# The last block of a four-layer cross-attention stack: outputs projected into rows, and the last unit's denominators partly on TensorE

## The chip, the cores and the metric

The kernel runs on one core of one Trainium2 chip. The metric is the device time of one execution in microseconds; the median of three runs is given. Beside it there is one profiled execution, whose span runs from the first to the last instruction.

## The reference

Four layers of multi-head cross-attention are applied one after the other to `x` (1 x 2048 queries x 256), with keys and values from a context of 1601 rows x 512. All is in float32.

```python
# layers L0, L2, L3: 16 heads of 64, two pairs of key columns with a bias from masks
q, k, v = hidden @ Wq, ctx @ Wk, ctx @ Wv            # split into heads
logits = einsum('bhqd,bhkd->bhqk', q, k) * 64 ** -0.5 + col_bias
out = softmax(logits) @ v                             # heads joined again: 1024 columns
x = out @ Wo + bo + x
# layer L1: 16 query heads of 16 on 4 key heads, on the rms-normed x, no bias
x = x + attention(rmsnorm(x) @ wq, ctx @ wk, ctx @ wv) @ wo
```

The output is `x` after L3.

## The kernel before

The sequences are held transposed: `xs` is x in SBUF with the 256 channels on partitions (two halves of 128) and the 2048 queries along the free dimension. The queries are cut into four query blocks b = 0 to 3 of 512 (`QB`, each `QT` = 4 pieces of 128), the keys into 13 chunks (`NT`) of 128 (the last has 65).

A layer with masks has 8 blocks of two heads (n = 0 to 7), the grouped layer L1 has 4 of four heads. One block and one query block make a `Unit`; there are 112, in the order layer, block, query block. Units 108 to 111 are the last block (layer 3, n = 7), and unit 111 is the very last. Each unit adds its heads' share of `out @ Wo` to `xs`.

A unit goes through stages, a chunk of keys at a time:
- `masked_scores` (L675): the two heads' scores of a chunk on TensorE into a pair of PSUM banks, which ScalarE copies to `p` (L687) while VectorE keeps a running maximum `top` (L692).
- `maxima` (L735, L736): after 13 chunks `top` is transposed by TensorE and reduced; `on_all_partitions` (L643, L646) sends the result to DRAM and back, spread over all partitions. `maxima_spread` copies it to the PSUM tile `b` (L751).
- `subtract` (L756, VectorE) and `masked_exp` (L761, ScalarE), in place in `p`; GpSimd adds `p` to `sums` chunk by chunk (L764 for the first, L766 for the rest).
- `values` (L801): the products of `p` with the values, summed over the chunks in the PSUM bank `po`; both heads lie in it, 64 partitions each. At the end `po` is copied to `oT` (L806).
- `denominators` (L822, L826, L827): `sums` is transposed in 8 pieces of 128 x 128 on TensorE, reduced and inverted on VectorE, and spread through DRAM into `by`. `divide` (L842, GpSimd) multiplies `oT` with it.
- `project` (L850): two products with `wo` into a pair of banks, which VectorE adds to `xs` (L862, or L857 with the bias `bo` in the layer's last block).
- After the last block `rows_out` transposes `xs` of a query block back into rows (L619), copies half on ScalarE and half on VectorE (L622, L623), and issues two output DMAs from SP (L625).

The order of work is written out by hand. A step is one chunk of one unit, and steps are taken in pairs. At step s, unit k scores chunk c where s = 13k + c; it exponentiates 18 steps later and takes the values 20 steps later. So at any time one unit is scored while the one before it is exponentiated. Shorter jobs are `Piece`s: `pieces.at(step, found)` puts them at a step, counted from a unit's last value chunk (step 13k + 32). Denominators come 2 steps later, division 5, projection 10 and `rows_out` 11. In the last block there are no projections of a next block to fill in between.

The instructions of TensorE, ScalarE and VectorE are tied to the order in which they are written. PSUM has two pair buffers (`psum.pair`), a third of the same size (`psum.b`), one bank `pm` and one bank `po`. Whatever wants a pair buffer waits until the reader of the one before last has finished. Unit 110's `sums`, `oT` and pieces share the engines with the exponentials of unit 111, behind which nothing more is scored.

Of the kernel before, what the change touches and what calls it, by code (L numbers as in the profile page):

```python
# [10 lines left out]
FP = mybir.dt.float32  # L11
# [3 lines left out]
ALU = mybir.AluOpType  # L15
# [3 lines left out]
P = 128  # L19
QB = 512  # L20
# [6 lines left out]
Piece = namedtuple("Piece", "run cost shared", defaults=(True,))  # L27
# [7 lines left out]
def tile_cross_attention_stack(ctx: ExitStack, tc: tile.TileContext, t: dict, out: bass.AP):  # L35
# [31 lines left out]
    nc = tc.nc  # L67
    x, cond = t["x"], t["ctx_2048"]
    _, S, C = x.shape
    _, T, CT = cond.shape  # L70
    NQ = S // P
    NC = C // P
    NCT = CT // P
    NB = S // QB
    QT = QB // P
    TCH = spans(T, P)
    NT = len(TCH)
# [3 lines left out]
    masked_names = ["L0_xattn_", "L2_xattn_", "L3_xattn_"]  # L81

    NP = 22
    const = ctx.enter_context(tc.tile_pool(name="const", bufs=1))
    weights = ctx.enter_context(tc.tile_pool(name="weights", bufs=2))
    heads = ctx.enter_context(tc.tile_pool(name="heads", bufs=2))
    probs = ctx.enter_context(tc.tile_pool(name="probs", bufs=NP))
    work = ctx.enter_context(tc.tile_pool(name="work", bufs=2))
# [3 lines left out]
    ps_m = ctx.enter_context(tc.tile_pool(name="ps_m", bufs=1, space=PSUM))  # L92
    scores_pools = ctx.enter_context(ExitStack())

    ident = const.tile([P, P], FP, name="ident")
    make_identity(nc, ident)
    ones = const.tile([P, P], FP, name="ones")
# [32 lines left out]
    psum = Scores()  # L130
# [3 lines left out]
    xs = const.tile([P, NB, NC, QB], FP, name="xs")  # L134
    x_rows = [probs.tile([P, QT, C], FP, name="p") for _ in range(NB)]
    for b in range(NB):
        nc.scalar.dma_start(
            out=x_rows[b], in_=x[0, ts(b, QB), :].rearrange("(n p) c -> p n c", p=P)
# [102 lines left out]
    def width(c):  # L241

        return sum(m for _, m in TCH[c : c + 2])

    def context_slice(c, held):

        a = TCH[c][0]
        n = width(c)
        ct = work.tile([P, NCT, 2 * P], FP, name="ct", bufs=3)
        nc.sync.dma_start(out=ct[:, :, :n], in_=ctxT_dram[:, :, a : a + n])  # L250
        held[c] = lambda k: ct[:, k, :n]
# [139 lines left out]
    class Masked:  # L391
# [5 lines left out]
        def __init__(self, l):  # L397
            self.l, self.name = l, masked_names[l]
# [59 lines left out]
    class Grouped:  # L458
# [5 lines left out]
        name = "L1_xattn_"  # L464
# [106 lines left out]
    layers = [Masked(0), Grouped(), Masked(1), Masked(2)]  # L571
# [11 lines left out]
    def keep(l, b):  # L583
        nc.sync.dma_start(out=xT_dram[l][b], in_=xs[:, b])
# [26 lines left out]
            (12, Piece(rms, 1.5)),  # L611
        ]

    def rows_out(b):

        pt = psum.pair((QT, C))
        for q in range(QT):
            for k in range(NC):
                nc.tensor.transpose(pt[:, q, ts(k, P)], xs[:, b, k, ts(q, P)], ident)  # L619
        rows = work.tile([P, QT, C], FP, name="ct", bufs=3)  # L620
        half = QT // 2
        nc.scalar.copy(rows[:, :half, :], pt[:, :half, :])  # L622
        nc.vector.tensor_copy(rows[:, half:, :], pt[:, half:, :])  # L623
        for q0 in (0, half):
            nc.sync.dma_start(  # L625
                out=out[0, b * QB + q0 * P : b * QB + (q0 + half) * P, :].rearrange(
                    "(n p) c -> p n c", p=P
                ),
                in_=rows[:, q0 : q0 + half, :],
            )  # L630

    def columns(q):

# [3 lines left out]
    def on_all_partitions(cols, to):  # L637


        n = cols.shape[1]  # L640
        rows = dram.tile([4, P, QT], FP, name="cols", bufs=4)[:n]
        with nc.allow_non_contiguous_dma(reason="1024 values, four at a time"):
            nc.sync.dma_start(out=rows.rearrange("h p q -> p h q"), in_=cols)  # L643
        for tile_, heads_ in to:
            src = rows[heads_].rearrange("(o h) p q -> o (h p q)", o=1)
            nc.sync.dma_start(out=tile_, in_=src.to_broadcast(tile_.shape))  # L646


    class Unit:
        def __init__(self, l, u, b, sub):  # L650
            self.l, self.u, self.b, self.sub = l, u, b, sub
            self.layer = u.layer
            self.pair = self.layer.SUBS[sub]
            self.masked = isinstance(self.layer, Masked)
            self.p = [None] * NT

        def rows(self, h):
            size = P // len(self.pair)
            return slice(size * h, size * h + size)
# [98 lines left out]
        def masked_exp(self, c):  # L758
            m = TCH[c][1]
            p = self.p[c]  # L760
            nc.scalar.activation(p[:m], p[:m], AF.Exp)  # L761
            if c == 0:
                self.sums = work.tile([P, 2, QB], FP, name="sums")
                nc.gpsimd.tensor_copy(self.sums, p)  # L764
            else:
                nc.gpsimd.tensor_tensor(self.sums[:m], self.sums[:m], p[:m], ALU.add)  # L766

        def scores_again(self, c, h, s):
# [17 lines left out]
        def values(self, c, part=None):  # L786


            u = self.u
            _, m = TCH[c]  # L790
            if c == 0 and not part:
                self.po = ps_o.tile([P, QB], FP, name="po")
            for h in range(len(self.pair)):
                r = self.rows(h)
                if self.masked:
                    to, v, p = self.po[r, :], u.v[:m, c, r], self.p[c][:m, h, :]
                else:
                    at = ts(part, QB // 2)
                    to, v = self.po[r, at], u.v[:m, c, :]
                    p = self.p[c][h // 2][:m, h % 2, at]  # L800
                nc.tensor.matmul(  # L801
                    to, v, p, start=(c == 0 and not part), stop=(c == NT - 1 and part != 0)
                )
            if c == NT - 1 and part != 0:
                self.oT = work.tile([P, QB], FP, name="oT", bufs=1)
                nc.scalar.copy(self.oT, self.po)  # L806

        @property
# [35 lines left out]
        def project(self):  # L844

            k = 0
            for py in psum.heads(False):
                of = range(k, k + py.shape[1])
                for k in of:
                    nc.tensor.matmul(  # L850
                        py[:, k - of[0], :], self.u.wo[:, ts(k, P)], self.oT, start=True, stop=True
                    )
                k += 1
                if self.masked and self.u.n == self.layer.BLOCKS - 1:
                    for j in of:
                        bo, to = bo_of[self.layer.l][:, j : j + 1], xs[:, self.b, j, :]
                        nc.vector.scalar_tensor_tensor(  # L857
                            to, py[:, j - of[0], :], bo, to, ALU.add, ALU.add
                        )
                else:  # L860
                    to = xs[:, self.b, of[0] : k, :]
                    nc.vector.tensor_tensor(to, py, to, ALU.add)  # L862

        def finish(self):

            last = 10 if self.masked else 8
            return [
                (2 if self.masked else 3, Piece(self.denominators, 1.0, not self.masked)),
                (5, Piece(self.divide, 0.0)), (last, Piece(self.project, 2.0, False)),
            ]  # L870
# [7 lines left out]
    units = []  # L878
# [4 lines left out]
    of = {}  # L883
# [14 lines left out]
    for i in range(NK):  # L898
        ct = first_context_slice(i)
# [63 lines left out]
    pieces = Pieces()  # L963

    def start_block(i):

        if i + 1 == len(blocks):
            return
        l, n = blocks[i + 1]
        layer = layers[l]  # L970
        nxt = made[l, n] = layer.load(n)

        loads, held = deque(), {}

        def chunks(make, cost):
            def piece(c):
                make(c, held[c])
                if loads:
                    loads.popleft()()

            loads.extend(lambda c=c: context_slice(c, held) for c in range(0, NT, 2))
            return [Piece(lambda c=c: piece(c), cost(c)) for c in range(0, NT, 2)]

        makers = layer.projections(nxt)
        first, second = [], []
        if makers:
            first = chunks(makers[0], lambda c: width(c) / P)
            second = chunks(makers[1], lambda c: float(len(TCH[c : c + 2])))
            for _ in range(3):
                loads.popleft()()  # L990
        first += layer.own_keys(nxt)
        second += layer.own_values(nxt)

        grouped = i and not isinstance(layers[blocks[i - 1][0]], Masked)
        (pieces.later if grouped else pieces.fill).extend(first)
        pieces.later.extend(second)

    def after(k):

        i, b, _ = units[k]  # L1000
        l, n = blocks[i]
        if n + 1 < layers[l].BLOCKS or not of[k].last:
            return []
        if l + 1 == len(layers):
            return [(11, Piece(lambda: rows_out(b), 1.0))]
        if isinstance(layers[l + 1], Masked):
            return [(11, Piece(lambda: keep(l + 1, b), 0.0))]
        return norm_factors(l + 1, b)
# [176 lines left out]
```

## Time and profile before

| what | value |
|---|---|
| median of 3 runs | 4948.83 us (4944.98 to 4951.98) |
| profiled execution | 4952.0 us, span 4950.3 us, mean granted TensorE clock 0.977 |
| busy, PE | 4747.6 us (96%) |
| busy, DVE | 3752.7 us (76%) |
| busy, ACT | 3218.1 us (65%) |
| busy, POOL | 2988.8 us (60%) |
| last score (L675) of unit 111 ends | 4875.3 us |
| last exponential (L761) ends | 4912.3 us |
| last addition to `sums` (L766) ends | 4927.7 us |

PE is TensorE's matmuls, PEld its weight loads, DVE VectorE, ACT ScalarE, POOL GpSimd, and SP the engine that issues nearly all DMAs. A float32 matmul has two records in the trace and a transpose one, so a projection of two products is "x4". Times in the trace count from the span's start. "L801" is a line of the kernel as printed above. The brackets at the end of a timeline row give the engine's idle time before the row and what ended it.

### The profile page before, as it was taken

What the parts mean: (1) busy time and instruction counts of PE and PEld (TensorE: products, weight loads), DVE (VectorE), ACT (ScalarE), POOL (GpSimd) and SP (SyncE); (2) the same over time, 40 slices, a digit from 0 to 9 for tenths busy, and PEclk for the clock granted to TensorE, in tenths of its full rate; (3) what the DMA queues carried; (4) which work ended last, traced back from release to release, by engine and by line L of the source; (5) the groups of instructions that cost most, each with busy time, mean ns of one, the idle gap of its engine ahead of it and who ended that gap; (6) DMA issues with size and microseconds to landing.
All of it is one profiled execution on the core that took longest, in us unless ns stands there. A gap on an engine that the chain in (4) does not pass through costs nothing.

```text
span 4950.3 us, 64060 instructions
## 1 busy us (share of the span) xinstructions
PE 4747.6 (96%) x24004; PEld 2061.6 (42%) x24004; DVE 3752.7 (76%) x3782; ACT 3218.1 (65%) x4000; POOL 2988.8 (60%) x1429
## 2 busy tenths in 40 slices
PE   6899999999999999999999999999999999999996
PEld 4344444444444444444344444444444444444432
DVE  3788888888765666554378888888888888888886
ACT  2677777777634555444467777777777777777774
POOL 1677777777720000000177777777777777777787
PEclk9999999999989999999799999999999999999998
DMA  4222222222201000012133232232222322223211
GB/s 140 65 79 81 80 83 82 81 85 75 71 26 37 19 19 19 26 29 59 29 91 87 77 86 79 82 88 77 78 85 84 84 82 78 79 83 86 78 29 34
DMA packets 352534, 337.88 MB, mean 68 GB/s; under 512 B 120697, under 2 KB 306297, under 8 KB 352224
## 3 DMA queue, kind: packets, MB, share of 16 engines
q1 hardware_dynamic: 348960, 328.41, 23.5%
q8 instruction: 189, 3.10, 0.3%
q0 software_dynamic: 1152, 3.28, 0.2%
q10 hardware_dynamic: 2112, 2.10, 0.1%
q14 instruction: 121, 0.99, 0.1%
HBM read 318.89 MB, written 14.82 MB: 67 GB/s over the span
## 4 chain that ended last, share of the span: by engine, by line
PE 85%; DVE 10%; issue 1%; POOL 1%; ACT 1%; DMA 1%; SPq 0%; POOLq 0%; DVEq 0%; ACTq 0%
PE po L801 27%; PE s L675 19%; PE t L706 8%; PE pm L381 6%; PE pm L427 6%; PE s L850 4%; PE pm L451 4%; PE t L771 3%; DVE rden L826 2%; DVE ntop L736 2%; PE s L822 2%; DVE xs L862 2%; PE s L735 2%; DVE top L692 1%; DVE p L756 1%
## 5 line engine op out<-in xcount | busy, mean ns | idle before, releaser
L766 POOL TENSOR_TENSOR sums<-sums,p 128x1024 f32<-128x1024 f32 (+1 forms) x1152 | 2726.6, 2367 | 754.0 <-ACT p L761 582.2
L687 ACT COPY p<-s 128x1024 f32<-128x1024 f32 (+1 forms) x1248 | 1235.0, 1014 | 680.5 <-PE s L675 590.5
L801 PE MATMUL po<-p,v 128*64 128x512 f32 (+3 forms) x8320 | 1512.2, 531 | 10.4 <-ACT p L761 6.7
L756 DVE TENSOR_TENSOR p<-p,b 128x1024 f32<-128x1024 f32 (+1 forms) x1248 | 1460.9, 1209 | 56.1 <-ACT b L751 54.9
L692 DVE TENSOR_TENSOR top<-s,top 128x1024 f32<-128x1024 f32 (+1 forms) x1056 | 1290.6, 1222 | 233.0 <-ACT p L687 169.6
L675 PE MATMUL s<-q,kT 64*128 64x512 f32 (+1 forms) x4992 | 1348.5, 634 | 91.8 <-DVE ntop L736 23.7
L761 ACT ACTIVATE p<-p 128x1024 f32<-128x1024 f32 (+1 forms) x1248 | 1254.9, 1057 | 51.7 <-DVE p L756 50.3
L801 PEld LDWEIGHTS po<-p,v 128*64 128x64 f32 (+3 forms) x8320 | 368.0, 126 | 1106.3 <-issue 865.3
L675 PEld LDWEIGHTS s<-q,kT 64*128 64x128 f32 (+1 forms) x4992 | 390.6, 182 | 741.8 <-issue 210.2
L783 ACT ACTIVATE p<-t 128x512 f32<-128x512 f32 (+1 forms) x760 | 412.3, 594 | 414.8 <-PE t L706 377.5
L719 DVE TENSOR_REDUCE row_top<-t 128x1 f32<-128x512 f32 x700 | 451.0, 686 | 260.4 <-PE t L706 257.7
L842 POOL TENSOR_TENSOR oT<-oT,by 128x512 f32<-128x512 f32 x112 | 142.9, 1275 | 764.5 <-DMA by<-cols 423.6
L706 PE MATMUL t<-kT,q 32*128 32x512 f32 (+1 forms) x1880 | 562.6, 642 | 0.0
L771 PE MATMUL t<-q,kT 32*128 32x512 f32 (+1 forms) x1520 | 493.7, 662 | 0.0
L706 PEld LDWEIGHTS t<-kT,q 32*128 32x128 f32 x1880 | 294.9, 316 | 168.8 <-issue 84.3
L381 PEld LDWEIGHTS pm<-wv,ct 128*128 128x128 f32 (+1 forms) x2496 | 290.2, 188 | 130.7 <-issue 71.2
L381 PE MATMUL pm<-wv,ct 128*128 128x128 f32 (+2 forms) x2496 | 322.5, 282 | 6.9 <-ACT v L385 3.2
L427 PE MATMUL pm<-ct,wk 128*128 128x256 f32 (+1 forms) x1288 | 301.1, 377 | 0.6 <-DMA wk<-in_L_xattn_Wk_dram 0.6
L736 DVE TENSOR_REDUCE ntop<-s 128x8 f32<-128x1024 f32 x96 | 117.5, 1224 | 229.0 <-PE s L735 229.0
L427 PEld LDWEIGHTS pm<-ct,wk 128*128 128x128 f32 x1288 | 221.0, 190 | 150.0 <-issue 93.6
L764 POOL COPY sums<-p 128x1024 f32<-128x1024 f32 x96 | 99.5, 1036 | 203.2 <-ACT p L761 203.2
L850 PE MATMUL s<-oT,wo 128*128 128x512 f32 x392 | 199.6, 632 | 17.5 <-POOL oT L842 13.6
(155 smaller groups left out, 2356.2 us busy)
## 6 DMA issues: line engine op xcount, KB each, us to landing
ct<-ctxT SPq DMA_DIRECT2D x288, 512.0 KB
xT<-xT SPq DMA_DIRECT2D x100, 512.0 KB
spread<-cols SPq DMA_DIRECT2D x96, 512.0 KB
by<-cols SPq DMA_DIRECT2D x192, 128.0 KB
xT<-xs SPq DMA_DIRECT2D x16, 512.0 KB
ct<-ctxT SPq DMA_DIRECT2D x48, 130.0 KB
wk<-in_L_xattn_Wk_dram SPq DMA_DIRECT2D x24, 256.0 KB
wv<-in_L_xattn_Wv_dram SPq DMA_DIRECT2D x24, 256.0 KB
```

The lines of the kernel that those rows point to most:

```text
L381: nc.tensor.matmul(pv[:md, d, :f], ct(k)[:, d * P : d * P + md], wv[:, k, :], start=(k == 0), stop=(k == NCT - 1),)
L427: nc.tensor.matmul(pk, u.wk[:, k, :], ct(k), start=(k == 0), stop=(k == NCT - 1))
L675: nc.tensor.matmul(s[:m, h, :], self.u.kT[r, a : a + m], self.q[r, :], start=True, stop=(a != TAIL),)
L687: nc.scalar.copy(p[:m], s[:m])
L692: nc.vector.tensor_tensor(self.top[:m], s[:m], self.top[:m], ALU.max)
L706: nc.tensor.matmul(s[:, at : at + n], self.q[r, columns(q)], self.u.kT[r, a : a + n], start=True, stop=True,)
L719: nc.vector.tensor_reduce(self.top[:, of, q, k : k + 1], s, AX.X, ALU.max)
L756: nc.vector.tensor_tensor(self.p[c][:m], self.p[c][:m], self.less[:m], ALU.add)
L761: nc.scalar.activation(p[:m], p[:m], AF.Exp)
L766: nc.gpsimd.tensor_tensor(self.sums[:m], self.sums[:m], p[:m], ALU.add)
L771: nc.tensor.matmul(s[:m], self.u.kT[r, a : a + m], self.q[r, :], start=True, stop=True)
L801: nc.tensor.matmul(to, v, p, start=(c == 0 and not part), stop=(c == NT - 1 and part != 0))
```

## The change

In the last block the residual is no longer updated in `xs`. For query blocks 0, 1 and 2, `rows_of_x` transposes `xs` into rows early in the block (steps 1406, 1416, 1442 as counted from the block's first step 1404) and ScalarE copies all of it. `project_rows` then takes `oT` as the stationary operand, so that its products (128 queries x 256 channels each) come out as rows; VectorE adds them to the rows, and two DMAs write them out. The bias `bo` of layer 3 is added one block earlier.

The very last unit differs more. GpSimd adds only chunks 0 to 5 to `sums`. For chunks 6 to 12, and at the end for `sums`, TensorE multiplies with a block of ones and adds up in the bank `pm` (`dens`), which gives the denominators on all partitions without a transpose or a trip through DRAM. `x_below` (step 1465) puts the rows of `xs` into PSUM with an identity product, where the projection is added later. `quarters` (step 1475, that of the last value chunk) inverts, multiplies, projects, copies and writes 128 queries at a time; between the multiplications and the projections it does the row projection of unit 110, which has been taken out of its place.

```diff
+    LAST_ADDED = 6
...
-    def rows_out(b):
+    def rows_of_x(b):
         pt = psum.pair((QT, C))
         for q in range(QT):
             for k in range(NC):
                 nc.tensor.transpose(pt[:, q, ts(k, P)], xs[:, b, k, ts(q, P)], ident)
-        rows = work.tile([P, QT, C], FP, name="ct", bufs=3)
-        half = QT // 2
-        nc.scalar.copy(rows[:, :half, :], pt[:, :half, :])
-        nc.vector.tensor_copy(rows[:, half:, :], pt[:, half:, :])
-        for q0 in (0, half):
-            nc.sync.dma_start(
...
+        x_rows_of[b] = work.tile([P, QT, C], FP, name="ct", bufs=3)
+        nc.scalar.copy(x_rows_of[b], pt)
+    x_rows_of = {}
+    def rows_out(b, rows, q, n):
+        nc.sync.dma_start(
+            out=out[0, b * QB + q * P : b * QB + (q + n) * P, :].rearrange(
+                "(n p) c -> p n c", p=P
+            ),
+            in_=rows[:, q : q + n, :],
+        )
...
+            self.final = self.l == len(layers) - 1 and u.n == self.layer.BLOCKS - 1
+            self.very_last = self.final and b == NB - 1
+            self.added = LAST_ADDED if self.very_last else NT
...
-            else:
+            elif c < self.added:
                 nc.gpsimd.tensor_tensor(self.sums[:m], self.sums[:m], p[:m], ALU.add)
...
+            if self.masked and self.very_last:
+                if c == 0:
+                    self.dens = ps_m.tile([P, QB], FP, name="pm")
+                todo = [self.p[c]] if c >= self.added else []
+                if c == NT - 1:
+                    todo.append(self.sums)
+                for p in todo:
+                    k = m if p is self.p[c] else P
+                    for h in range(2):
+                        nc.tensor.matmul(
+                            self.dens[self.rows(h), :], ones[:k, :64], p[:k, h, :],
+                            start=(c == self.added), stop=(p is self.sums),
+                        )
             if c == NT - 1 and part != 0:
-                self.oT = work.tile([P, QB], FP, name="oT", bufs=1)
+                if self.masked and self.very_last:
+                    self.oT = work.tile([P, 2, QB], FP, name="spread", bufs=1)[:, 0, :]
+                else:
+                    self.oT = work.tile([P, QB], FP, name="oT", bufs=1)
                 nc.scalar.copy(self.oT, self.po)
...
-                if self.masked and self.u.n == self.layer.BLOCKS - 1:
+                if self.masked and self.u.n == self.layer.BLOCKS - 1 - (self.l == len(layers) - 1):
...
+        def project_rows(self, py=None):
+            py = py or psum.pair((QT, C))
+            for q in range(QT):
+                nc.tensor.matmul(
+                    py[:, q, :], self.oT[:, ts(q, P)], self.u.wo, start=True, stop=True
+                )
+            rows = x_rows_of[self.b]
+            nc.vector.tensor_tensor(rows, py, rows, ALU.add)
+            for q in (0, QT // 2):
+                rows_out(self.b, rows, q, QT // 2)
+        def x_below(self):
+            pairs = [psum.pair(), psum.pair()]
+            self.py = [pairs[q // 2][:, q % 2, :C] for q in range(QT)]
+            for q in range(QT):
+                for k in range(NC):
+                    nc.tensor.matmul(
+                        self.py[q][:, ts(k, P)], xs[:, self.b, k, ts(q, P)], ident,
+                        start=(k == 0), stop=False,
+                    )
+        def quarters(self, before):
+            rden = work.tile([P, NC, QB], FP, name="xT")[:, 0, :]
+            for q in range(QT):
+                nc.vector.reciprocal(rden[:, ts(q, P)], self.dens[:, ts(q, P)])
+                nc.gpsimd.tensor_tensor(
+                    self.oT[:, ts(q, P)], self.oT[:, ts(q, P)], rden[:, ts(q, P)], ALU.mult
+                )
+            before.project_rows(psum.b().rearrange("p a (b c) -> p (a b) c", c=C))
+            rows = work.tile([P, QT, C], FP, name="ct", bufs=3)
+            for q in range(QT):
+                nc.tensor.matmul(
+                    self.py[q], self.oT[:, ts(q, P)], self.u.wo, start=False, stop=True,
+                )
+                nc.scalar.copy(rows[:, q, :], self.py[q])
+                rows_out(self.b, rows, q, 1)
         def finish(self):
+            if self.very_last:
+                return [(0, Piece(lambda: self.quarters(of[len(units) - 2]), 2.0))]
+            if self.final:
+                found = [
+                    (2, Piece(self.denominators, 1.0, False)), (5, Piece(self.divide, 0.0)),
+                ]
+                if self.b < NB - 2:
+                    found.append((10 - 2 * self.b, Piece(self.project_rows, 2.0, False)))
+                return found
...
     def start_block(i):
         if i + 1 == len(blocks):
+            start = units.index((i, 0, 0)) * NT
+            for b, at in enumerate((2, 12, 38, NB * NT + 9)):
+                piece = Piece(lambda b=b: rows_of_x(b), 1.0, False)
+                if b == NB - 1:
+                    piece = Piece(lambda: of[len(units) - 1].x_below(), 2.0, False)
+                pieces.at(start + at, [(0, piece)])
             return
...
         if l + 1 == len(layers):
-            return [(11, Piece(lambda: rows_out(b), 1.0))]
+            return []
```

More of the change, by code (lines that the diff above doesn't have):

```diff
@@ L619, in rows_out @@
                 nc.tensor.transpose(pt[:, q, ts(k, P)], xs[:, b, k, ts(q, P)], ident)
-        rows = work.tile([P, QT, C], FP, name="ct", bufs=3)
-        half = QT // 2
-        nc.scalar.copy(rows[:, :half, :], pt[:, :half, :])
-        nc.vector.tensor_copy(rows[:, half:, :], pt[:, half:, :])
-        for q0 in (0, half):
-            nc.sync.dma_start(
[L626 to L630, printed above, removed]
+        x_rows_of[b] = work.tile([P, QT, C], FP, name="ct", bufs=3)
[8 more added lines that the diff above has]
+        )
     def columns(q):
```

## The prediction

> **What bounds the kernel now.** I read the granted clock first (0.977, one core), then the slices of the page: PE is at 9 tenths in all 40 but the first two and the last, so what ends the span must be looked for in the last slices. A table of stretches near the end (its columns: length, then the busy time of PE, weight load, DVE, ACT and POOL with the number of instructions, granted clock, DMA share, GB/s):
>
> ```profile
> 4860.00:4880.00 20.00, 16.38 (x74) 5.64 (x70) 18.40 (x17) 14.99 (x16) 15.41 (x8) 1.00 0.08 17
> 4880.00:4900.00 20.00, 13.77 (x58) 4.19 (x58) 14.71 (x14) 11.79 (x13) 18.67 (x10) 1.00 0.19 53
> 4900.00:4920.00 20.00, 12.86 (x43) 3.39 (x41) 10.81 (x11) 9.17 (x9) 19.53 (x9) 0.83 0.05 13
> 4920.00:4951.00 31.00, 11.18 (x36) 5.67 (x36) 5.24 (x8) 1.75 (x3) 8.76 (x5) 0.61 0.13 43
> ```
>
> DVE leads until 4880 (18.40 of 20), POOL from there to 4928 (19.53 of 20), and after that no engine is busy for half the time. The chain of waits says the same in order (start, length, what):
>
> ```profile
> 4925.40 2.35 POOL sums L766
> 4927.79 2.00 PE s L822 x8
> 4929.81 1.24 DVE rden L826
> 4931.30 2.53 DMA cols<-rden
> 4934.39 2.89 DMA by<-cols
> 4938.76 3.80 PE s L850 x4
> 4944.04 1.77 PE s L619 x7
> ```
>
> So the end is two pieces. POOL adds up the last unit's thirteen chunks (one copy, then 2.4 us each) until 4927.74, although its last exponential was there at 4912.3. Then nine dependent links take 4950.3 - 4927.8 = 22.5 us: transposes, reduction, a trip of the denominators through DRAM (6.1 us), division, projection, transposes, two copies, write. The timeline of the same end:
>
> ```profile
> 4894.40 0.69 DVE L623 COPY ct<-s 128x512 f32<-128x512 f32 x1 [1.60 <-ACT ct L622]
> 4897.45 17.07 POOL L766 TENSOR_TENSOR sums<-sums,p 128x1024 f32<-128x1024 f32 x7 [0.52 <-ACT p L761]
> 4900.77 1.22 DVE L826 TENSOR_REDUCE rden<-s 128x8 f32<-128x1024 f32 x1 [1.17 <-PE s L822]
> 4904.47 6.74 PE L801 MATMUL po<-p,v 128*64 128x512 f32 x24 [1.86 <-ACT p L761]
> 4915.79 3.78 PE L850 MATMUL s<-oT,wo 128*128 128x512 f32 x4 [4.59 <-POOL oT L842]
> ```
>
> The third matters too: the next-to-last unit's projection (L850) waits for its division on POOL, and the last unit's value products stand behind it in PE's order.
>
> **The Trainium skill.** Its page TensorE: Matmul & The Clock Gate (section "Part 1: The HAM clock gate (the "warmup" mystery)") says that TensorE falls to half clock after an idle window of some 3.4 us. The trace agrees: after an idle stretch of 4.6 us the four records of L850 take 3.78 us, not 1.98. TensorEngine Tiling (Array Packing) (section "Overview") says that products with 64 output columns can run two at a time; here the two heads' L801 products, four records, take 1.94/2 = 0.94 to 0.97 us a chunk in a run of two chunks, while one full-width product of the same length takes 1.98/2 = 0.99 (L850). VectorE: DVE Perf Modes ("First, the fixed hardware budget") has the reciprocal as an iterated division, repeated 8 times. The trace agrees that it is slow for each element:
>
> ```profile
> L605 DVE RECIPROCAL rms<-rms 128x4 f32<-128x4 f32 x4 | 0.7, 178 | 1.1 <-ACT rms L604 1.1
> L827 DVE RECIPROCAL rden<-rden 128x8 f32<-128x8 f32 x96 | 19.5, 203 | 3.3
> L834 DVE RECIPROCAL rden<-pm 128x16 f32<-128x16 f32 x16 | 4.1, 257 | 34.3 <-PE pm L831 34.3
> ```
>
> From 4 to 16 elements 178 to 257 ns: 6.6 ns each. A 128x128 one is thus 257 + 112 x 6.6 = 1.0 us, no shape of the trace. Below it can't be under the 0.2 us of L827; above, 8 cycles an element at the page's 0.96 GHz (its section "Specifications") and 0.15 start give an estimate of 1.2. I take 1.0.
>
> **Part 1, ahead of the end.** Three `rows_of_x` calls go in at steps 1406, 1416, 1442: 8 transposes (1.1 us, L619), one ACT copy of 1024 (1.01, L687), and one of the two pair buffers held for both. At 1406 they stand before the projection L850, which then waits: its buffer comes at 4741.7 and not 4740.5, DVE's update follows, +1.25. At 1416 and 1442 they stand before the transposes of the maxima (L735), for which DVE already waits 1.57 us: +1.15 each. Sum +3.6; 0 if PE's gaps take them, 6.3 if copy and transposes add up each time. ACT has 5 us free in 20, so its copy delays no exponential much.
>
> The bias goes into block n=6's projections: two DVE operations of 0.70 in place of one of 1.22, +0.2 for the three that fall in the DVE-led last block, +0.6 (0 to 0.8).
>
> Query block b=0's write-out at step 1447 goes. DVE there waited 1.69 us for ACT's half, copied 0.69 and its update was 0.2 longer: -2.5, of which I take -2.4. Its four row products have as many columns as the two of L850 that they replace. Its two output DMAs move a step ahead; SP's next DMA behind them is issued 11 us later, so they cost nothing. Net by 4879: +1.8.
>
> Query block b=1 goes from steps 1459/1460 to 1457. Before, DVE idled 1.91 us for L850 and spent 1.41; now the update (1.22) stands between chunks 9 and 10 with a wait of some 0.4. That is -1.7, so the last subtraction of b=2 ends at 4890.5, as before. Then the stall and copy of L623 (DVE 4892.8 to 4895.0) are gone too: chunks 1 to 4 are subtracted by 4897.2, not 4899.6. SP: b=1's output DMAs go behind those of the last maxima, already under way.
>
> **Part 2, the last unit.** POOL ends b=2's sums at 4895.9 + 1.8 = 4897.7 (it had no gap from 4877 on, so it keeps the delay). L822 1.2, reduction and reciprocal 1.4: 4900.3. `x_below` wants both pair buffers, one of them free only then: 16 records of 128 columns cost 2.05 us (L381 has the same shape), half before, half after: PE free at 4901.2. Behind it wait the value products of chunks 3 to 12.
>
> From there PE has 10 chunks of values and 8 pairs of `dens` products (chunks 6 to 12 and `sums`), of L801's shape: 18 x 0.935 (1.87 a pair of chunks in the chain) = 16.8 us, **T0 = 4918.0**. DVE subtracts chunks 5 to 12 by 4909.4 and ACT is 1.1 behind, so PE and no longer POOL leads. POOL does one copy, five additions and b=2's division (1.0 + 12.0 + 1.3) by 4912. The price of the `dens` products not running two at a time is 16 x 0.98 - 7.5 = +8.
>
> **Part 3, after T0.** DVE: four reciprocals 4.1, then b=2's row update 1.22 (L862), T0+5.4; PE's four row products for it (2.0) lie beside the reciprocals. POOL: 128 columns cost 0.44 (2.37 for 1024, 1.26 for 512); PE 0.5 a quarter, ACT 0.37 (L385's 256 columns): the last quarter is copied at T0+6.0. SP then has b=2's two DMAs ahead of the four quarters: all six wait for DVE's update behind the reciprocals. Issue 0.38 each (L625's median) and a gap of 0.03: the last starts at T0+7.5. Before, the last issue began at 4947.2 and the span ended 3.1 later. **End T0+10.6 = 4928.6**, against 4950.3: -21.7. The trip through DRAM, L822, L619 and three of four copies are gone. What is late next: PE until T0, then DVE's reciprocals and SP's queue.
>
> The profiled execution took 4952.0, its span and 1.7 around it, 3.2 above the median of 4948.83. I subtract the difference from the median: 4927.
>
> **Rivals.**
> - PE pays more (0.12): `dens` not two at a time, or half clock for some 8 us of the end. T0 + 8, time 4935. The clock of 0.83 in 4900 to 4920 speaks for it; that the products fill the idle stretches which brought it down speaks against.
> - More gain (0.10): the three insertions hide, as does the bias (-4.2), and a cheap reciprocal lets b=2's rows go at T0+3.3: time 4921.
> - PE at half clock from the last unit's first values on (0.06). The same list doubled: values 3.9, L822 2.0, `x_below` 4.1, 18 x 1.87 = 33.7: T0 = 4938.8, end about 4950. No change.
> - **Slower** (0.03): the same mechanism from 4860 on. PE was busy 16.4 us of 4860 to 4880 and 11 of the 16 after, so doubling adds 12.8 and 6 to the case above: span end 4969, time 4967. It decides at the point where the clock falls: before about 4895 the change loses. Against it: those slices show 1.00 under the same load, and the change adds PE work.
> - The likeliest, as summed (0.69): 4927.
>
> **Numbers.** About 0.2%, 10 us, is what a measurement of this kernel can tell from no change. The first, second and last cases are faster by more: 0.91; no change 0.06; slower 0.03. Range: below, the case of more gain and half of the 7 us between the three runs shown: 4917. Above, the dearer PE with 2 more for the insertions: 4937.
>
> **What would show it.** Right: six POOL additions and copies, not thirteen, in the last unit; PE without gaps from `x_below` to the last `dens` at clock 1.00, T0 near 4918; reciprocals of about 1.0 us; the last six output DMAs within 3 us, the last started 3 us before the end; no transit of `cols` after 4910. Wrong: a half-clock PE there, reciprocals of 0.3, maxima of b=0 to b=2 later by more than 2 us each, or POOL the last releaser of the `dens`.

## The result, and the profile after

The changed kernel takes 4922.55 us (median of 6 runs, 4918.1 to 4925.97) against 4947.5 for six runs of the kernel before: ratio 0.9948, interval 0.9935 to 0.9961, so 19 to 32 us less. A later pair of measurements gave 0.9959 (0.9946 to 0.9971). Predicted were 4927 against 4948.83, or -21.7. The profiled execution took 4920.88 us, its span 4918.4.

The same stretches as before, though this execution is already 8 us ahead here (columns: length, busy time and instructions of PE, weight load, DVE, ACT and POOL, granted clock, DMA share, GB/s):

```profile
4860.00:4880.00 20.00, 15.87 (x69) 5.74 (x70) 18.06 (x17) 11.47 (x12) 18.14 (x9) 1.00 0.24 66
4880.00:4900.00 20.00, 17.71 (x82) 6.73 (x80) 16.01 (x16) 14.76 (x16) 19.37 (x10) 0.91 0.05 15
4900.00:4919.00 19.00, 12.53 (x56) 5.30 (x52) 5.29 (x6) 3.92 (x7) 4.30 (x6) 0.93 0.16 55
```

Where POOL had 19.53 of 20 us after 4900, it has 4.30 of 19; PE has work for 12.53 and a granted clock of 0.93. The end of the chain of waits (start, length, what; rows of `issue` are left out):

```profile
4889.15 1.18 PE s L847 x8
4890.36 1.24 DVE rden L851
4891.64 1.16 PE s L907 x8
4892.80 3.58 PE po L809 x16
4896.38 0.86 PE pm L822 x4
4897.24 0.86 PE po L809 x4
...
4906.68 1.72 PE pm L822 x8
4908.40 1.92 PE b L893 x8
4910.32 0.45 PE s L923 x2
4910.79 0.38 ACT ct L926
4911.31 1.12 PE s L923 x4
```

L847 is `denominators` of unit 110, L907 `x_below`, L809 the values, L822 the `dens` products, L893 `project_rows`, L923 the last projection. PE has no gap from 4892.80 to the last `dens` at 4908.40, and neither POOL nor a transit of `cols` is in the chain any more. The timeline of the finish:

```profile
4908.45 3.39 DVE L916 RECIPROCAL xT<-pm 128x128 f32<-128x128 f32 x4 [7.63 <-PE pm L822]
4911.19 4.24 SPq L628 DMA_DIRECT2D out_dram<-ct  x6
4911.31 1.10 PE L923 MATMUL s<-wo,spread 128*128 128x256 f32 x4 [0.55 <-ACT ct L926]
4911.76 1.16 DVE L897 TENSOR_TENSOR ct<-b,ct 128x1024 f32<-128x1024 f32 x1
4912.97 0.67 PE L923 MATMUL s<-wo,spread 128*128 128x256 f32 x2 [0.55 <-ACT ct L926]
```

Four reciprocals take 3.39 us (each alone 0.89 to 0.96; they overlap a little). The second and fourth product each wait 0.55 us for ScalarE, which is copying the other half of the same PSUM pair.

**How the experiments are read.** Whole runs spread over 8 us here and over up to 21 us in the runs below, more than most parts are worth. The trace has better marks: the reductions of the maxima on DVE (`ntop`). Unit 107's comes just before the last block scores anything. Where nothing was changed and the clock held, stretches between these marks agree within 0.02 us from run to run. Spans are printed to a tenth, so one that ends with the span is good to 0.05. In us, from start to start:

| stretch | before | after |
|---|---|---|
| start of the span to maxima of unit 107 | 4732.19 | 4723.18 |
| 107 to 108 | 38.33 | 40.68 |
| 108 to 109 | 34.47 | 34.66 |
| 109 to 110 | 38.33 | 39.37 |
| 110 to 111 | 36.91 | 34.36 |
| 111 to the end | 70.07 | 46.15 |
| 107 to the end | 218.11 | 195.22 |

So the change is worth 22.9 us in this pair of profiles. The other 9.0 of their difference were there before the last block began: comparing the reductions of all units one by one, they arise in the first 300 us and between units 31 and 48, in stretches that the change leaves alone; from unit 48 to 106 the two kernels agree within 0.3 us. In the other runs of this document, which are alike up to there but for the bias of some units, unit 107's maxima start anywhere from 4713.7 to 4735.7.

### The profile page after: what moved, and what is told of

It reads as the page before. It is cut to its first block, busy times and chain, and to the rows that moved or that the text cites. A ratio compares the mean times of both kernels' runs of the same rounds, so it can differ in the third digit from the quotient of the medians.

```text
span 4918.4 us, 64148 instructions
## 1 busy us (share of the span) xinstructions
PE 4733.3 (96%) x24052; PEld 2062.8 (42%) x24052; DVE 3751.4 (76%) x3779; ACT 3219.9 (65%) x4003; POOL 2973.4 (60%) x1425
## 4 chain that ended last, share of the span: by engine, by line
PE 86%; DVE 10%; issue 1%; ACT 1%; DMA 1%; POOL 1%; SPq 0%; another core or an unknown queue 0%; DVEq 0%; ACTq 0%; POOLq 0%
PE po L809 27%; PE s L683 19%; PE t L714 8%; PE pm L382 6%; PE pm L428 6%; PE pm L452 4%; PE s L875 4%; PE t L779 3%; DVE rden L851 2%; DVE ntop L744 2%; PE s L847 2%; DVE xs L887 2%; PE s L743 2%; DVE top L700 1%; DVE p L764 1%
## 5 line engine op out<-in xcount | busy, mean ns | idle before, releaser
L774 POOL TENSOR_TENSOR sums<-sums,p 128x1024 f32<-128x1024 f32 x1145 | 2710.5, 2367 | 749.2 <-ACT p L769 577.7
L809 PE MATMUL po<-p,v 128*64 128x512 f32 (+3 forms) x8320 | 1503.7, 528 | 5.5 <-ACT oT L831 2.9
L809 PEld LDWEIGHTS po<-p,v 128*64 128x64 f32 (+3 forms) x8320 | 367.1, 126 | 1090.5 <-issue 859.0
L759 ACT COPY b<-spread 128x1024 f32<-128x1024 f32 x96 | 97.5, 1015 | 149.3 <-DVE p L764 148.5
```

The costliest lines, as they stand in the source:

```text
L809: nc.tensor.matmul(to, v, p, start=(c == 0 and not part), stop=(c == NT - 1 and part != 0))
```

## The experiments

**1. Rows only.** All four query blocks are projected into rows; the last unit's sums, denominators and finish stay as before.

```diff
-            self.very_last = self.final and b == NB - 1
+            self.very_last = False
...
-                if self.b < NB - 2:
-                    found.append((10 - 2 * self.b, Piece(self.project_rows, 2.0, False)))
+                at = 10 - 2 * self.b if self.b < NB - 2 else 10
+                found.append((at, Piece(self.project_rows, 2.0, False)))
...
-                if b == NB - 1:
-                    piece = Piece(lambda: of[len(units) - 1].x_below(), 2.0, False)
```

> Rows for all four query blocks of the last block, but the very last unit keeps its thirteen additions on POOL, its denominators through DRAM and one projection of 512 queries at the end. From the maxima reduction of unit 107 to the end: before 218.1 us, after the change 195.2. Theory (the gain lies in the last unit's denominators): about -2 against before: 216, of which +1 up to the maxima of unit 111 as in the changed kernel, and at the end -2.6 for the transposes and copies behind the projection (L619, L622, L623). Rival (the row projection brings most of it): under 205. Whole time: 0.9995 of before against 0.997 or less.

Measured: 149.05 us from 107 to 111, 67.32 from there, 216.37 in all; ratio 0.9992 (0.9982 to 1.0002). The rival that the rows bring most of it is out: alone they are worth 1.7 us.

**2. The last unit only.** Query blocks 0 and 1 keep the old projection, bias and write-out.

```diff
-                    found.append((10 - 2 * self.b, Piece(self.project_rows, 2.0, False)))
+                    found.append((10, Piece(self.project, 2.0, False)))
...
-            for b, at in enumerate((2, 12, 38, NB * NT + 9)):
+            for b, at in ((2, 38), (3, NB * NT + 9)):
...
-            return []
+            return [(11, Piece(lambda: rows_out_old(b), 1.0))] if b < 2 else []
```

> The very last unit and unit 110 as in the changed kernel; query blocks 0 and 1 keep the old projection into xs, with the bias there, and the old write-out. Theory: from the maxima of unit 107 to those of unit 111 about 149 us, as in the changed kernel, since the insertion at steps 1406 and 1416 (+2.35 by unit 108) and the gain of blocks 0 and 1 cancel; from there to the end 48.5, 2.4 more than the 46.15 of the changed kernel, because block 1's write-out stalls DVE again and unit 111's first values come later. Total 197.5, -20.6 against before. Rival (row projection brings most): over 210.

Measured: 202.82; ratio 0.9967 (0.9956 to 0.9978). That is 5 more than expected, and the stretches say where: 109 to 110 took 43.30, not 39.4, and 111 to the end 49.59. In the first of them TensorE's clock fell, in work that is the same in both kernels:

```profile
4825.00:4830.00 5.00, 4.70 (x12) 0.89 (x12) 4.79 (x6) 3.35 (x4) 3.34 (x2) 0.67 0.00 0
4830.00:4835.00 5.00, 4.32 (x12) 1.48 (x12) 3.35 (x3) 2.57 (x4) 3.04 (x2) 0.50 0.00 0
4835.00:4840.00 5.00, 5.00 (x22) 1.90 (x20) 2.62 (x3) 3.85 (x4) 2.93 (x2) 0.80 0.00 0
```

(Columns as above.) Some 10 us below full clock cost 3.9. Without that the kernel is at 198.9, 19 below the kernel before: most of the gain is the last unit's, as the theory had it. The last stretch has a fall too, of 6.8 us where the changed kernel has one of 3.4 there, so 19 is rather too low. The two halves, 1.7 and 19, leave 1 to 2 us that only both together bring; the theory puts it down to block 1's write-out ahead of unit 111's first values, which no run takes out alone. Such falls turn up in other runs below, and are taken out by name where they do.

**3. All additions on POOL.** Only the product of `sums` with ones is left on TensorE.

```diff
-    LAST_ADDED = 6
+    LAST_ADDED = 13
...
-                            start=(c == self.added), stop=(p is self.sums),
+                            start=(c == min(self.added, NT - 1)), stop=(p is self.sums),
```

> LAST_ADDED 13: POOL adds all thirteen chunks of the very last unit as before; only the product of sums with ones is on TensorE, in place of transposes, reduction and the trip through DRAM. Theory: POOL is the last again, 12 additions of 2.44 and unit 110's division after 4889.1 in the time of the changed kernel give 4919.7, and with the product, at half clock after the idle time, the dens are ready 13 to 14 us later than the 4908.4 of the changed kernel; from the maxima of unit 107 to the end 208 to 210, 8 to 10 less than before. So shifting the additions to TensorE is worth some 13 of the 23, the rest is the shorter way behind them. Rival (the sums were covered, only the way behind them counted): no more than 3 us behind the changed kernel, 198.

Measured: 209.56; ratio 0.9991 (0.9982 to 0.9999). As the theory said: 14.3 behind the changed kernel (15.4 if that one's fall of the clock, shown under runs 4 to 6, is taken out), 8.6 ahead of the one before. The timeline shows the old wait, and the price of the idle time: the last pair of products takes twice the 0.94 to 0.97 that the prediction read for a chunk.

```profile
4919.35 12.01 POOL L774 TENSOR_TENSOR sums<-sums,p 128x1024 f32<-128x1024 f32 x5
4931.40 1.97 PE L822 MATMUL pm<-sums,ones 128*64 128x512 f32 x4 [17.32 <-POOL sums L774]
```

**4 to 6. Nine, three and seven additions.** Only `LAST_ADDED` differs (and the `start` of the run before).

> LAST_ADDED 9: three more additions on POOL, three fewer pairs of products on TensorE. Theory: TensorE set the time of the dens in the changed kernel with POOL 6 us ahead; three more additions of 2.44 make POOL the last: its chunk 8 ends at 4909.8 in that kernel's time, the dens are ready 2.3 later than there, the end is 2.3 later: 48.5 from the maxima of unit 111. Rival (POOL has nothing to say): 2.6 earlier, 43.6.

> LAST_ADDED 3: POOL adds chunks 0 to 2 only, TensorE has three more pairs of products. Theory (TensorE without gaps sets the time of the dens): 3 x 0.86 = 2.6 later, 48.7 from the maxima of unit 111 to the end, against 46.15 in the changed kernel. Rival (the last exponential and the way behind it set it): 46.2.

> LAST_ADDED 7: one more addition on POOL. POOL's last addition ends 2.4 later than in the changed kernel, still some 4 us ahead of TensorE. Theory: one pair of products less, 0.86 earlier, 45.3 from the maxima of unit 111. Rival (POOL already binds at 7, as it did at 9, where 50.5 was measured): 46.5 or more.

Measured from the maxima of unit 111: nine 50.49, three 47.75, seven 45.39. Nine is worse by more than expected, since PE idles 5.06 us for POOL and the product of the sums and those behind it run at half clock:

```profile
4917.19 2.34 POOL L774 TENSOR_TENSOR sums<-sums,p 128x1024 f32<-128x1024 f32 x1
4919.58 1.98 PE L822 MATMUL pm<-sums,ones 128*64 128x512 f32 x4 [5.06 <-POOL sums L774]
4921.48 3.07 PE L893 MATMUL b<-wo,oT 128*128 128x256 f32 x8
```

Three seems only 1.6 worse. But the changed kernel's own 46.15 holds a fall of the clock, which begins 13 us behind those maxima, where PE has been waiting for unit 111's first exponentials; twelve records take 4.51 us in it and 2.98 in run 4, where the clock stays up:

```profile
4884.64 4.51 PE L809 MATMUL po<-p,v 128*64 128x512 f32 x12 [0.82 <-ACT oT L831]
```
```profile
4894.50 2.98 PE L809 MATMUL po<-p,v 128*64 128x512 f32 x12 [0.82 <-ACT oT L831]
```

From the maxima of unit 111 to the last `dens` it is 36.15 in the changed kernel and 36.13 in run 8, both with the fall, 35.11 in run 7 without it, and 37.69 with three additions, also without: 2.58 more, three pairs of 0.86. With seven, and the fall, it is 35.42, or 0.7 less. So TensorE sets the time up to seven additions, and at nine POOL does; the crossing lies between. Both rivals are out.

**7. The finish in one piece** instead of 128 queries at a time, with two copies and two DMAs.

```diff
-            for q in range(QT):
-                nc.vector.reciprocal(rden[:, ts(q, P)], self.dens[:, ts(q, P)])
-                nc.gpsimd.tensor_tensor(
-                    self.oT[:, ts(q, P)], self.oT[:, ts(q, P)], rden[:, ts(q, P)], ALU.mult
-                )
+            nc.vector.reciprocal(rden, self.dens)
+            nc.gpsimd.tensor_tensor(self.oT, self.oT, rden, ALU.mult)
...
+            for q in range(0, QT, 2):
+                pair = self.pairs[q // 2][:, :, :C]
+                nc.scalar.copy(rows[:, q : q + 2, :], pair)
+                rows_out(self.b, rows, q, 2)
```

> The changed kernel without the finish 128 queries at a time: one reciprocal of 128x512, one multiplication of 128x512, four products, two copies and two DMAs for the very last unit. Theory (the four pieces overlap): behind the dens reciprocal 3.3, multiplication 1.3, products 2.0, two copies 1.2, issue 0.4 and 3.1 to the end, 11.2 against the 10.0 of the changed kernel, so 47.4 from the maxima of unit 111. Rival (reciprocals and SP's queue set the pace anyway): within 0.3 of 46.15.

Measured 45.88, by the total even a little better than the changed kernel, as the rival had it and against the theory. But that run had no fall of the clock there, and the changed kernel's 46.15 has one. From the last `dens` (4910.23) to the end (4921.0) it is 10.77, against 10.00 (4908.40 to 4918.4): the pieces of 128 are worth 0.8 us and not the 1.2 expected. The timeline shows a reason why it is so little, though no run tests it alone: unit 110's update goes before the multiplication ends, so its DMAs are no longer behind.

```profile
4910.28 3.36 DVE L915 RECIPROCAL xT<-pm 128x512 f32<-128x512 f32 x1 [7.63 <-PE pm L822]
4913.55 1.16 DVE L897 TENSOR_TENSOR ct<-b,ct 128x1024 f32<-128x1024 f32 x1
4913.77 1.27 POOL L916 TENSOR_TENSOR spread<-spread,xT 128x512 f32<-128x512 f32 x1 [8.41 <-issue]
4914.74 3.37 SPq L628 DMA_DIRECT2D out_dram<-ct  x4
```

**8. The insertions two steps later.**

```diff
-            for b, at in enumerate((2, 12, 38, NB * NT + 9)):
+            for b, at in enumerate((4, 14, 40, NB * NT + 9)):
```

> The three rows_of_x two steps later: 1408, 1418, 1444, pairs of steps without a projection and without maxima. Theory (an insertion costs because another job wants the same pair buffer in the same pair of steps): unit 107's maxima to unit 108's 38.4 and unit 109's to unit 110's 38.4, as before the change (38.33 each), not 40.7 and 39.4; from 107 to 111 146.0 against 149.07. Rival (TensorE's 1.1 us are paid wherever they stand): 149.

Measured: 38.84 to unit 108, 34.99, 42.48 and 34.73; 151.04 in all. The third holds a fall of the clock (0.50 for some 10 us). The combined kernel below has the same insertions and no such fall: 38.85, 34.98, 38.53, 34.73, together 147.09, 2.0 less than the changed kernel. So the place counts, but it isn't free. Set against the kernel before in the first stretch and against the changed kernel in the second and fourth, which the later insertions have moved into, they cost 0.5, 0.3 and 0.4. The third stretch has no insertion any more and still takes 0.2 more than before: that is the bias (see the point on it below), and the first 0.5 has such a share too. Without the bias the three insertions cost about 1 us here, and about 3 at the old steps. The theory had 146 for the whole, the rival 149.

**9. The finish in another order.** Pieces 0, 2, 1, 3, so that the next product is in the other PSUM pair, and unit 110's rows written from ScalarE's queue after the last copy.

```diff
+            order = (0, 2, 1, 3)
...
-            for q in range(QT):
+            for q in order:
...
+            write()    # unit 110's two output DMAs, with nc.scalar as their queue
```

> The changed kernel with the four pieces of the finish in the order 0, 2, 1, 3, so that a product never goes into the PSUM pair that ScalarE is just copying from, and unit 110's two output DMAs issued from ScalarE's queue after the last copy, not on SP behind the quarters. Theory (after the dens the end is set by product, copy, product in one PSUM pair, and by six DMAs in one queue): 1.2 less from the end of the dens to the end, 8.8 against 10.0 in the changed kernel. Rival (the reciprocals pace it): within 0.3 of 10.0.

Measured: 9.06 from the last `dens` to the end (4913.94 to 4923.0), 0.9 less than 10.00; 8.8 was expected. The waits of PE for ScalarE's copies are gone. The run changes two things at once: counted from the last `dens`, the last copy ends 0.5 earlier (5.1 for 5.6), and the last DMA is issued 1.3 earlier (5.3 for 6.5). What each would bring alone was not tried.

**10. The changed kernel again, and all of it together** (finish, seven additions, later insertions), five rounds each on one chip.

> The changed kernel once more, for the size of the effect on this chip and to see its stretches again: 149.05 from the maxima of unit 107 to those of unit 111, and from there 45.1 or 46.15, as TensorE's clock does or does not fall to half once when it waits for unit 111's first exponentials; each fall elsewhere in the block adds about 4. Ratio to before 0.995.

> The finish of the run before, LAST_ADDED 7, and the insertions at steps 1408, 1418, 1444. Sum of the parts: -2.2 for the insertions, -0.86 for the seventh chunk, -1.2 for the finish: 190 us from the maxima of unit 107 to the end, where the changed kernel has 194.2 without any fall of the clock. Ratio to before some 0.0009 below that of the changed kernel, which five rounds may not tell from it; the stretches of the trace can.

The changed kernel: 4928.65 us, ratio 0.9959 (0.9946 to 0.9971); 155.30 and 45.11. The 155.30 holds two falls of the clock (+4.0 to unit 108, +2.3 to unit 110); the 45.11 has none. The combined kernel: 4923.03, ratio 0.9940 (0.9928 to 0.9952); 147.09 and 44.52, where the last still holds a fall worth some 1.2. Its total of 191.6 against 195.22 and 200.41 is as expected from the parts; the two ratios overlap, so the runs alone don't tell it from the changed kernel.

## Why the prediction was right, point by point

- **What bounds the end: right.** POOL's additions and the links behind them were the end; run 3 splits the gain into 14.3 for the additions taken from POOL and 8.6 for the rest of the change (15.4 and 8.6, or 24 in all, without the fall of the clock in the changed kernel). That PE would lead from `x_below` on is shown by runs 5 and 6.
- **Insertions, +3.6: about 3.0.** The stretches that hold them took 2.35 more (to unit 108, the first two) and 1.04 more (to unit 110, the third), but each also holds a bias of some 0.2. The reason given, another job for the pair buffers in the same pair of steps, is borne out by runs 8 and 10 for two thirds of it; some 1 us is paid at the later steps too.
- **The bias, +0.6: right.** It shows wherever nothing else was changed: 0.19 in the stretches that end at units 107 and 109, and 0.20 in the one that ends at 110 once run 10 has moved the insertion out of it. In run 2, where blocks 0 and 1 keep the old bias, the stretches to 107 and 108 do not grow by more than 0.02. The stretch to 108 with the new bias alone was not run; at the same 0.2 the three after unit 107 make 0.6.
- **Query block 0, -2.4: measured -2.55** (110 to 111). Net from unit 107 to 111: +1.0 for +1.8, most of the difference in the insertions.
- **POOL's end for unit 110:** 15.7 behind the maxima of unit 111 predicted (4897.7 - 4882.0), 15.75 measured. PE, not POOL, then released L847 1.1 later, because the clock fell; the prediction had the fall only as a rival for the end.
- **18 pairs at 0.935: mis-sized.** In one unbroken run they cost 0.86 each, 15.6 for 16.8 in all. They also began later, 20.5 behind the maxima instead of 19.2, and 1.0 of that is the fall. The two errors cancel: the last `dens` came 36.15 behind the maxima, with 36.0 predicted, and that closeness is luck.
- **Reciprocals of 1.0: a little too dear,** 0.89 to 0.96 each and, as they overlap, 3.39 for four where 4.1 was taken. From 16 to 512 elements the cost is 257 to 3360 ns, 6.3 ns each. The estimate of 1.2 us, worked out from the Trainium skill's page VectorE: DVE Perf Modes (sections "First, the fixed hardware budget" and "Specifications"), was further off.
- **SP's order: wrong.** I had unit 110's DMAs ahead of the quarters. In the program they come behind: the DVE update ends at 4912.9, and the last issue starts at 4914.9. And I had no wait of a product for a copy in the same PSUM pair. Still the end came after 10.0 and not 10.6: the last issue began at 6.5 instead of 7.5, behind cheaper reciprocals, and the end followed 3.5 and not 3.1 later. That two wrong links gave nearly the right sum is luck as well.
- **The signs.** The six output DMAs began within 3.7 us and not 3. Maxima later by over 2 us were named as a sign of being wrong, and those of blocks 0 to 2 came 2.35, 2.5 and 3.6 late in all; but the prediction's own sum has 2.4 for the first, so the sign was badly set.
- **The clock in the kernel before: misread in part.** The prediction read the half clock of L850 as the effect of 4.6 us of idle time. In that trace the clock is at half from 4913.0 on, 1.8 us into the idle stretch; more on this below.
- The sum: -22.9 in the profiles from unit 107 on, for -21.7.

## What to carry to other kernels

At the end of a kernel, look for the engine that finishes last after its inputs are there, and give part of its work to one that idles; the split is best where both finish together, and past that point the idle engine pays again, for its clock drops. Measure parts of a microsecond between marks within the trace that the change leaves in place, not by whole runs, and look at the granted clock of each stretch before reading a difference. Where a job is put into a pipeline with few buffers, choose a step without another job for the same buffer.

## What the runs showed of the hardware

TensorE's clock fell to half in the middle of the last block although no gap in its work there was near the 3.4 us that the prediction took from the Trainium skill's page TensorE: Matmul & The Clock Gate (section "Part 1: The HAM clock gate (the "warmup" mystery)"). Where the two differ, the measurement decides. In the second run of the changed kernel it fell after a gap of 1.64 us (a line of the timeline, then two stretches with the columns as above):

```profile
4740.13 1.13 PE L683 MATMUL s<-q,kT 64*128 64x512 f32 x4 [1.64 <-DVE top L700]
4738.01:4741.43 3.42, 1.61 (x8) 0.30 (x4) 3.32 (x4) 3.42 (x5) 0.87 (x1) 1.00 0.00 0
4741.43:4744.84 3.41, 3.38 (x8) 0.80 (x8) 3.36 (x3) 1.95 (x2) 2.48 (x2) 0.50 0.00 0
```

The first profile of the same kernel has the same gap and no fall:

```profile
4740.92 1.13 PE L683 MATMUL s<-q,kT 64*128 64x512 f32 x4 [1.63 <-DVE top L700]
4738.71:4742.12 3.41, 1.71 (x8) 0.30 (x4) 3.31 (x4) 3.41 (x4) 0.77 (x1) 1.00 0.00 0
4742.12:4745.54 3.42, 2.60 (x10) 0.70 (x12) 3.42 (x4) 3.10 (x5) 2.58 (x2) 1.00 0.00 0
```

The stretches are not cut at will. In each of the 13 traces all changes of the granted clock lie on one grid of 3.413 us, to within 0.004, and where the grid stands against the work differs from run to run. (In the first profile it is counted back from the change at 4885.48, 42 steps.) Take the emptiest step of the grid at this place, between the maxima of units 107 and 108: the clock fell after it in the four profiles where PE was busy for 1.57 to 1.69 us of it, and held in the nine with 1.71 to 2.31. From 109 to 110 it fell in four with 1.57 to 1.64 and held in nine with 1.77 to 2.13. So at these two places the clock falls after a step that is less than half busy. The border is rough, since the ends of matmuls are modelled in the trace. Behind the maxima of unit 111 this is not so clean: the clock fell after 1.92 in the changed kernel and held after 1.64 in the kernel before, so busy time is not the whole of it.

In the middle of the block a fall lasts two or three steps, some 7 or 10 us, and costs 2 to 4. Between the maxima of 107 and 108 four of nine profiles with an insertion at step 1406 had it, and none of four without. The insertion need not be the cause: in the kernel before, the 3.41 us from 4746.33 hold only 1.58 us of PE work, and its grid happened to cut there at 4745.76, where it is 1.78.
